# Sampling and feed-forward work redistributed in a fused convolution, attention and feed-forward kernel

## The chip, the cores and the metric

The kernel runs on one core of one Trainium2 chip. Its engines are TensorE (PE, with its weight loads as PEld), VectorE (DVE), ScalarE (ACT), GpSimd (POOL) and SyncE (SP, which here issues most DMAs); each runs its own queue of instructions in order, and they meet at semaphores. The metric is the device time of one execution in microseconds (us), the median of several. Below, "idle" of an engine is time in which its next instruction waits.

## What is computed

The input is four images of 64 x 64 tokens with 256 channels in 32-bit floats. For each image:

```
x = x + deformable_conv(group_norm(x))        # 8 groups x 9 points, bilinear samples, mask, 256x256 out
t = tokens(x)                                 # 4096 x 256
t = t + additive_attention(layer_norm(t))     # alpha = sum_u Wa[u] * tanh(q[u] + k[u] + bh[u]), 32 units
t = t + ffn(layer_norm(t))                    # only the 2047 tokens with the largest weight t.wr + br
                                              # gelu(x w1 + b1) w2 + b2, times that weight
```

The convolution samples by offsets. The kernel splits it into a dense part (for each of 25 window places, a plane of weights times the shifted image, added up) and exact rows for those tokens whose offsets leave the window (gathered one by one).

In the attention the sum over tanh is a function of 4096 x 4096 pairs of tokens. The kernel works it out as sums of quotients: a matmul gives a denominator `d`, ACT takes its logarithm and the exponential of the negative (that is 1/d), another matmul gives a numerator `nn`, DVE multiplies them, and three such products of each pair are added up, before the softmax's own exponential.

The feed-forward sorts the chosen tokens by scattering the rows of all tokens to a table in memory, reads this back in four chunks of 512 rows, runs the two matmuls with the gelu between them, and scatters the results to the output.

## The kernel before

The stages, in the order of the profiled execution: the offsets and weights of all four images (`offsets_and_weights`); the dense sampling of image 0 alone; then for each image n a mixed stage, in which the feed-forward of image n-1, the attention's preparation for n and the first steps of the sampling of n+1 take turns, and the attention of n, which carries the rest of the sampling of n+1 on its DVE; at the end the feed-forward of the last image.

*The attention.* It walks 256 tiles: 8 blocks of 512 queries by 32 blocks of 128 keys. Its order is written by hand in four lanes, one for each engine, with a lag in tiles for each operation. Of one tile, PE makes D1 to D3 (denominators, L878) and N1 to N3 (numerators, L888); ACT takes L1 to L3 (logarithms, L961), E1 to E3 (exponentials, L963) and W (the softmax's exponential, L899); DVE takes six products (L893, "m1a" to "m3b"), "s3b" (L971) and "sum" (L974); POOL takes two additions, "s12" (L967) and "s3a" (L969). After every eight tiles PE multiplies the weights by the values (L915), and DVE adds the result to a running sum ("out", L935). On DVE's lane stand also "side", which in each tile takes one step of the sampling, and "again", which takes a second step in some tiles: as many as there are steps over 256, evenly spread over the tiles.

```
[("m1a", 1), ("m1b", 1), ("m2a", 1), ("side", 0), ("s3b", 2), ("again", 1), ("m2b", 1), ("sum", 2),
 ("m3a", 1), ("m3b", 1), ("out", 3)],
[("s12", 1), ("s3a", 1)],
```

At the end of each block of queries, four "out" slots each finish one row of 128 tokens: the reciprocal (L939), the load of the residual `tr` (L941), the division with its addition (L943), the store (L944), the row's statistics (L746, L747) and its dot product with `wr` (L753), all in one tile (`hand_over`, L922). In the middle of each block, `queries` (L864) makes `qn` for the block after it, two operations of 128x512 on DVE.

*The sampling.* `sample_image` is a generator. One step is a multiply of 128x1024 (L684) or an addition of 128x1024 (L692), each with a `yield` after it. The weight planes `wb` come by DMA (L675). After each quarter of the tokens four pairs of rows go through PE (L705) and out, with an addition of the bias `outb` (L709) and of PE's result (L712) on DVE. When `S.gather` is set, `next(single, None)` advances the generator `exact_rows` inside the multiply's step, so that the gathers on POOL (L618), and the gathered rows' multiply (L629, 128x1152) and reduce (L630), fall into the same tile as the multiply L684. `STEPS` is the number of steps that one image's sampling is taken to have. A single PSUM bank is shared between the values' matmul and the sampling; `bank_taken` tells.

*The feed-forward.* `feed_forward` (L1212) searches the k-th largest weight on DVE, scatters 32 blocks of rows (L1263, POOL's queue), writes the plain rows (`base`, L1276, ACT), and then takes four chunks. A chunk reads its rows `xs` (L1287, POOL's queue), makes `si`, scales the rows into `vs` (L1296, ACT), transposes them into `xT` (L767 and L768), prepares the residual (L1302 on POOL, L1304 on DVE), then runs `ph` (L1312) with the gelu (L1313), and `py` (L1317) with L1320 and the scatter of results (L1324). In the mixed stages its pool "row" has one buffer, so xs, vs and xT are single; in the last feed-forward it has two. `hT`, the gelu's output, has two halves in a tile that takes the place of the tokens' tile once those are read. In the mixed stages the vector operations of the feed-forward and of the preparation go through `pinned`, and show as L257.

*The turns.* A string decides in which order the three generators of a mixed stage advance: m is the feed-forward, o the preparation, s the sampling.

```
turns = "ommm" + "mo" * 5 + "moooo" + "mss" + "oss" * 12 + "m" + ("ossss" * 3 + "msss" * 4) * 4
```

Of the kernel before, what the change touches and what calls it, by code (L numbers as in the profile page):

```python
# [12 lines left out]
ALU = mybir.AluOpType  # L13
# [19 lines left out]
STEPS = 412  # L33
# [12 lines left out]
def layers_kernel(ctx: ExitStack, tc: tile.TileContext, a, out: bass.AP):  # L46
# [51 lines left out]
    tdot = const.tile([P, NT], F32, name="tdot")  # L98
# [134 lines left out]
    S = SimpleNamespace(bank=True, wants=False, gather=True)  # L233
# [327 lines left out]
    def exact_rows(n, uf, out_rows):  # L561

        ui = S.smp.tile([P, 1], I32, tag="ui", name="ui")
# [20 lines left out]
        )  # L584

# [5 lines left out]
        nc.vector.tensor_scalar(pos, pos, 0.0, 65.0, ALU.max, ALU.min)  # L591

# [11 lines left out]
        nc.vector.tensor_copy(ti, gt)  # L604

# [8 lines left out]
        for g in range(G):  # L614
            ga = S.dn.tile([P, K2, 2, 2, CG], F32, tag="ga", name="ga")
            for s in range(K2):
                for dy in range(2):
                    keep(nc.gpsimd.indirect_dma_start(  # L618
                        out=ga[:, s, dy].rearrange("p c e -> p (c e)"), out_offset=None, in_=tab_d[n],
                        in_offset=bass.IndirectOffsetOnAxis(  # L620
                            ap=ti[:, dy, g * K2 + s : g * K2 + s + 1], axis=0
                        ),
                    ))
                yield
            for _ in range(2):
# [4 lines left out]
            keep(nc.vector.tensor_reduce(  # L630
                so[:, g : g + 1, :].rearrange("p g e -> p (g e)"),
                ga.rearrange("p s r c e -> p e (s r c)"), AX.X, ALU.add,
            ))
            yield
# [7 lines left out]
        nc.vector.tensor_copy(sT, pt)  # L642
        pm = S.ps_m.tile([P, C], F32, tag="pm", name="pme")
# [12 lines left out]
    def sample_image(n, depth=1):  # L656
# [3 lines left out]

        uf = yield from list_tokens(n)
# [3 lines left out]
        for c in range(L // CH):  # L665
            ac = S.dn.tile([P, CC, CH], F32, tag="ac", name="ac", bufs=min(depth, 2))
            for f in range(CC):
                xs = S.dn.tile([P, CH // W + 4, MP], F32, tag="xs2", name="xs2", bufs=min(depth, 2))
                o = c * (CH // W) * MP
                nc.sync.dma_start(  # L670
                    out=xs.rearrange("p r w -> p (r w)"), in_=xp_d[n][f, :, o : o + (CH // W + 4) * MP]
                )
                for d in range(ND):
                    wb = S.dn.tile([P, CH], F32, tag="wb", name="wb", bufs=2 * depth)
                    nc.sync.dma_start(  # L675
                        out=wb, in_=wt_d[n][f, d : GH * ND : ND, c * CH : (c + 1) * CH].partition_broadcast(CG)
                    )
# [12 lines left out]
                    yield  # L690
                    if d > 0:
                        keep(nc.vector.tensor_add(ac[:, f, :], ac[:, f, :], pr))  # L692
                        yield
            for i in range(0, CH // P, 2):
                while bank_taken():
                    if S.gather:
                        next(single, None)
                    yield
# [10 lines left out]
                keep(nc.vector.tensor_add(  # L709
# [5 lines left out]
                )  # L715
                yield
        for _ in single:
            yield
        put_rows(n, *exact[0])

# [27 lines left out]

    def weight_sums(i, row):

        row_stats(tmv[:, i, :], row)
        pr = S.sb.tile([P, C], F32, tag="tr", name="pr")
        nc.vector.scalar_tensor_tensor(pr, row, 1.0, wr, ALU.mult, ALU.mult, accum_out=tdot[:, i : i + 1])  # L753
# [96 lines left out]
    def attention(n, v, kf, beside, steps):  # L850
# [8 lines left out]
        def queries(q):  # L859
# [3 lines left out]
            for blk in range(2):  # L863
                nc.vector.tensor_scalar(qn[:, blk, :], qf[:, blk, :], csel[:, blk : blk + 1], None, ALU.mult)  # L864
# [31 lines left out]
        ets, acc, pend, due = {}, {}, [], []  # L896
# [25 lines left out]
        def hand_over():  # L922

            if not due:
                return
# [23 lines left out]
        second = min(max(steps - nb, 0), nb)  # L949
        rs, ds, ns = {}, {}, {}  # L950

        def emit(op, b):

            p = int(op[1]) if op[1:2].isdigit() else 0
# [84 lines left out]
        while pend or due:  # L1039
# [6 lines left out]
    def attention_any(n):  # L1046

        num = nc.values_load(wide[0:1, n : n + 1], min_val=0, max_val=2)
        with tc.If(num > 0), scope(
# [116 lines left out]
            for i in range(NT):  # L1166
                weight_sums(i, v[:, i, :])
# [44 lines left out]
    def feed_forward(n, vec):  # L1212
# [8 lines left out]

        r = inv_std(S.one, tmv[:, :, 1], NT, "lnr2")
# [47 lines left out]

# [13 lines left out]
        hT2 = S.one.tile([P, 2, FF // P, 512], F32, tag="big", name="hT")  # L1284
        for s in range(NSORT // 512):
            xs = S.row.tile([P, 4, C + 4], F32, tag="xs", name="xs")
            get = nc.gpsimd.dma_start(  # L1287
# [6 lines left out]
            vs = S.row.tile([P, 4, C], F32, tag="vs", name="vs")  # L1294
# [12 lines left out]
            yield  # L1307
            hT = hT2[:, s % 2]
            for f in range(FF // P):
# [3 lines left out]
                nc.scalar.activation(hT[:, f, :], ph, AF.Gelu_apprx_tanh, bias=b1[:, f, :])  # L1313
            for t in range(4):
# [13 lines left out]
                if t < 3:  # L1328
                    yield
# [23 lines left out]
    for n in range(NB):  # L1353
        with scope(("att", 1, 0), ("smp", 2, 0), ("dn", 1, 0)):
# [5 lines left out]
            with scope(  # L1360
                ("one", 1, 0), ("two", 2, 0), ("sb", 2, 0), ("row", 1, 0), ("rp", 3, 0),
# [16 lines left out]
            with scope(  # L1378
# [3 lines left out]
                attention(n, v, kf, [sampling], STEPS - turns.count("s") if n + 1 < NB else 0)  # L1382
# [42 lines left out]
```

## Time and profile before

| | |
|---|---|
| median of 3 runs | 10,845.07 us (10,837.85 to 10,854.71) |
| the profiled execution | 10,899.14 us, of which the trace's span is 10,897.4 us |
| busy in the span | PE 9,186.4 us (84%), DVE 8,586.7 (79%), ACT 7,381.2 (68%), POOL 5,001.3 (46%) |
| mean granted TensorE clock | 0.897 |

The profiled execution is one run with the profiler on, and lies 54 us above the median. Windows of it, with times from the span's start:

| stage | from, to (us) | length |
|---|---|---|
| offsets and weights of all images | 0, 812 | 812 |
| sampling of image 0 | 812, 1477 | 665 |
| preparation of attention 0 | 1477, 1580 | 103 |
| attention 0 with sampling of image 1 | 1580, 3657 | 2077 |
| rest of it, then mixed stage 1 | 3657, 4080 | 423 |
| attention 1 with sampling of image 2 | 4080, 6066 | 1986 |
| mixed stage 2 | 6083, 6466 | 383 |
| attention 2 with sampling of image 3 | 6466, 8456 | 1990 |
| mixed stage 3, without sampling | 8473, 8781 | 308 |
| attention 3, without sampling | 8781, 10675 | 1894 |
| feed-forward of image 3 | 10675, 10898 | 223 |

In a group's line of the profile stand the source line, the engine, the operation, output and inputs with their shapes, the count, then the busy time in us and the mean of one in ns, and at the end the engine's idle time just before these instructions and what ended it. In a line of the stage table each engine has its busy time in the window and its number of instructions; then come the granted clock, the DMA's busy share and GB/s.

### The profile page before, as it was taken

The page shows a single profiled execution, that of the slowest core. Times are in us where ns is not written, and L with a number is a line of the kernel's source. Part 1 is how long each engine was busy: PE and PEld are TensorE (multiplying, and loading weights), DVE is VectorE, ACT ScalarE, POOL GpSimd, SP SyncE. Part 2 cuts the span into 40 slices and gives each one's busy share as a digit, 9 for nine tenths or more (in the row PEclk, how much of TensorE's full clock was granted, in tenths as well). Part 3 has the DMA queues.
Part 4 walks back from the last instruction along what each step waited for, and adds up shares of the span by engine and source line. Part 5 has one row for each costly group of instructions (what it writes and reads, how often), then busy time and mean ns, then how long its engine had stood idle before and what let it go on. Part 6 is the DMA issues. An engine that isn't in the chain of part 4 may idle for free. (4 is left out here: it accounts for less than half of the span.)

```text
span 10897.4 us, 115889 instructions
## 1 busy us (share of the span) xinstructions
PE 9186.4 (84%) x38460; PEld 4477.6 (41%) x38460; DVE 8586.7 (79%) x13502; ACT 7381.2 (68%) x8388; POOL 5001.3 (46%) x2947
## 2 busy tenths in 40 slices
PE   7871049999999679999999679999999699999996
PEld 4541014444444344444444344444444344444444
DVE  7767879898999668888888668888888357777772
ACT  4440027777888428888888338888888378888882
POOL 0004216665555316666555226666555145555552
PEclk8985569999999779999999789999999799999998
DMA  3336642221111351222111442212111300000002
GB/s 116 120 130 194 212 141 63 59 63 57 62 57 59 122 160 50 52 51 51 51 50 45 141 129 51 52 49 51 50 50 40 103 13 8 8 8 7 7 5 74
DMA packets 375187, 766.02 MB, mean 70 GB/s; under 512 B 49104, under 2 KB 204400, under 8 KB 374544
## 3 DMA queue, kind: packets, MB, share of 16 engines
q1 hardware_dynamic: 315984, 670.26, 19.1%
q0 software_dynamic: 32448, 54.39, 3.2%
q10 hardware_dynamic: 26112, 33.56, 0.9%
q8 instruction: 310, 5.08, 0.2%
q14 instruction: 333, 2.73, 0.1%
HBM read 580.88 MB, written 177.14 MB: 70 GB/s over the span
## 5 line engine op out<-in xcount | busy, mean ns | idle before, releaser
L893 DVE TENSOR_TENSOR r<-nn,r 128x512 f32<-128x512 f32 x6144 | 3942.0, 682 | 1119.7 <-PE nn L888 1066.9
L888 PE MATMUL nn<-qn,kf 32*128 32x512 f32 (+1 forms) x12288 | 4486.1, 646 | 281.1 <-DVE r L893 243.3
L967 POOL TENSOR_TENSOR r<-r 128x1024 f32<-128x1024 f32 x1024 | 2725.0, 2661 | 3062.9 <-DVE r L893 3003.8
L961 ACT ACTIVATE r<-d 128x1024 f32<-128x1024 f32 x3072 | 3117.8, 1015 | 1269.3 <-DVE r L971 833.4
L878 PE MATMUL d<-qf,kf 32*128 32x512 f32 (+1 forms) x12288 | 3376.3, 638 | 63.7 <-ACT r L961 59.4
L963 ACT ACTIVATE r<-r 128x1024 f32<-128x1024 f32 x3072 | 3124.1, 1051 | 32.6
L915 PE MATMUL pv<-v,et 128*128 128x257 f32 x8192 | 2241.4, 420 | 18.1 <-DVE acv L935 18.1
L888 PEld LDWEIGHTS nn<-qn,kf 32*128 32x128 f32 (+1 forms) x12288 | 1398.8, 188 | 2008.3 <-DVE r L893 1530.7
L915 PEld LDWEIGHTS pv<-v,et 128*128 128x128 f32 x8192 | 1591.4, 204 | 1042.8 <-issue 801.6
L878 PEld LDWEIGHTS d<-qf,kf 32*128 32x128 f32 (+1 forms) x12288 | 1024.9, 187 | 1337.8 <-issue 800.2
L969 POOL TENSOR_TENSOR r<-r 128x512 f32<-128x512 f32 x1024 | 1311.5, 1281 | 184.6 <-DVE r L893 111.9
L692 DVE TENSOR_TENSOR ac<-ac,prd 128x1024 f32<-128x1024 f32 x768 | 968.2, 1261 | 9.4
L684 DVE TENSOR_TENSOR prd<-xs,wb 128x1024 f32<-128x1024 f32 x768 | 954.0, 1242 | 20.9 <-DMA wb<-wt 18.8
L618 POOL DMA_INDIRECT ga<-tab,tii x576 | 660.6, 1147 | 223.8 <-issue 118.6
L899 ACT ACTIVATE et<-et,nshift 128x512 f32<-128x512 f32 x1024 | 723.7, 707 | 26.6 <-DVE et L974 26.6
L971 DVE TENSOR_TENSOR r<-r 128x512 f32<-128x512 f32 x1024 | 699.9, 684 | 2.7 <-POOL r L967 2.6
L974 DVE TENSOR_TENSOR et<-r 128x512 f32<-128x512 f32 x1024 | 696.7, 680 | 3.6 <-POOL r L969 3.5
L116 ACT ACT_TABLE_LOAD x9 | 11.5, 1283 | 844.3 <-DVE mv L257 692.4
L705 PE MATMUL pmo<-outwp,ac 128*128 128x256 f32 x512 | 148.2, 443 | 473.7 <-DVE ac L692 433.6
L1324 POOL DMA_INDIRECT out_dram<-vs,si x64 | 74.6, 1165 | 563.3 <-DVE vs L257 386.5
L478 POOL MEMSET w<- 128x1600 f32 x16 | 22.9, 1432 | 675.0 <-DVE red L454 385.9
L705 PEld LDWEIGHTS pmo<-outwp,ac 128*128 128x128 f32 x512 | 108.4, 221 | 527.3 <-DVE ac L692 315.6
(343 smaller groups left out, 5446.3 us busy)
## 6 DMA issues: line engine op xcount, KB each, us to landing
wb<-wt SPq DMA_DIRECT2D x800, 512.0 KB
tab<-tb SPq DMA_DIRECT2D x128, 256.0 KB
v<-t SPq DMA_DIRECT2D x64, 512.0 KB
xs<-xp SPq DMA_DIRECT2D x32, 680.0 KB
xp<-xp SPq DMA_DIRECT2D x32, 544.0 KB
xt<-in_x_dram SPq DMA_DIRECT2D x32, 512.0 KB
xr<-in_x_dram SPq DMA_DIRECT2D x64, 256.0 KB
t<-xr SPq DMA_DIRECT2D x64, 256.0 KB
```

The source lines that it names most:

```text
L684: keep(nc.vector.tensor_tensor(pr.rearrange("p (r w) -> p r w", w=W), src, wb.rearrange("p (r w) -> p r w", w=W), ALU.mult,))
L692: keep(nc.vector.tensor_add(ac[:, f, :], ac[:, f, :], pr))
L878: keep(nc.tensor.matmul(d[:, j, :], kf[g, blk, rows(kt)], qs[q][0][g, blk, :], start=True, stop=True))
L888: keep(nc.tensor.matmul(nn, kf[g, blk, rows(kt)], qs[q][1][g, blk, :], start=True, stop=True))
L893: keep(nc.vector.tensor_tensor(r[:, j, :], ns[j], r[:, j, :], ALU.mult))
L899: keep(nc.scalar.activation(ets[b], ets[b], AF.Exp, bias=nshift))
L915: keep(nc.tensor.matmul(pv, ets[b0 + i][:, rows(j)], v[:, k0 + i, :], start=(i == 0), stop=(i == PVB - 1)))
L961: keep(nc.scalar.activation(rs[b, p], ds.pop((b, p)), AF.Ln))
L963: keep(nc.scalar.activation(rs[b, p], rs[b, p], AF.Exp, scale=-1.0))
L967: keep(nc.gpsimd.tensor_tensor(rs[b, 1], rs[b, 1], rs[b, 2], ALU.add))
L969: keep(nc.gpsimd.tensor_tensor(rs[b, 1][:, 0], rs[b, 1][:, 0], rs[b, 3][:, 0], ALU.add))
L971: keep(nc.vector.tensor_add(rs[b, 1][:, 1], rs[b, 1][:, 1], rs[b, 3][:, 1]))
```

## The change

1. *Pieces of the sampling.* `exact_rows` yields True where its next piece is to have a step of its own; `sample_image` then runs it after the addition's step (`while own`). The gathered rows' multiply and its reduce, now in two halves, the start of the list and the projection at its end are such pieces. Waiting for the bank no longer advances the gather.
2. *Second steps by what is left.* `S.left` counts the steps that remain, from `STEPS` = 440 (412 before). "again" adds to an account what is left, shared among the tiles left, and takes a second step when this reaches one.
3. *Row ends in pieces.* `hand_over` makes the sum at once, and queues the division and the statistics, which run one at a time in "out" slots that have no sum. `tr` and `tt` have four buffers.
4. *Engines.* `qn` and the addition of `outb` go from DVE to POOL.
5. *The dot product with `wr`* leaves the attention for the start of `feed_forward`, which makes it in 32 operations from the loaded tokens.
6. *The chunks' rows.* A function `chunk(s)` fetches and prepares the rows. xs and vs have two places each inside the large tile, whose hT is now single; chunk s+1 is prepared after the second `py` of chunk s. xs is issued by SP. xT has two buffers in the mixed stages too.
7. *Turns* follow the new yields; the first m, with the loads of the feed-forward, comes before the first o.

```diff
-STEPS = 412
+STEPS = 440
...
+            yield
+            yield True
             gf = ga.rearrange("p s r c e -> p (s r c) e")
             wv = wg[:, g * K2 : (g + 1) * K2].rearrange("p s r (c o) -> p (s r c) o", o=1)
             keep(nc.vector.tensor_tensor(gf, gf, wv.to_broadcast([P, 4 * K2, CG]), ALU.mult))
-            keep(nc.vector.tensor_reduce(
-                so[:, g : g + 1, :].rearrange("p g e -> p (g e)"),
-                ga.rearrange("p s r c e -> p e (s r c)"), AX.X, ALU.add,
-            ))
+            for e in (slice(0, CG // 2), slice(CG // 2, CG)):
+                yield True
+                keep(nc.vector.tensor_reduce(
+                    so[:, g, e], ga[..., e].rearrange("p s r c e -> p e (s r c)"), AX.X, ALU.add,
+                ))
             yield
...
-                    if S.gather:
-                        next(single, None)
+                    S.left -= 1
+                    own = S.gather and next(single, None)
                     yield
                     if d > 0:
                         keep(nc.vector.tensor_add(ac[:, f, :], ac[:, f, :], pr))
+                        S.left -= 1
+                        yield
+                    while own:
+                        own = next(single, None)
+                        S.left -= 1
                         yield
...
-                keep(nc.vector.tensor_add(
+                keep(nc.gpsimd.tensor_add(
                     xr, xr, outb.rearrange("p (o c) -> p o c", o=1).to_broadcast([P, 2, C])
                 ))
...
-                nc.vector.tensor_scalar(qn[:, blk, :], qf[:, blk, :], csel[:, blk : blk + 1], None, ALU.mult)
+                keep(nc.gpsimd.tensor_scalar(qn[:, blk, :], qf[:, blk, :], csel[:, blk : blk + 1], None, ALU.mult))
...
             if not due:
+                if rest:
+                    if len(rest) == late[0]:
+                        late[0] -= 1
+                    rest.pop(0)()
                 return
...
-                es = S.sb.tile([P, 1], F32, tag="es", name="es")
-                nc.vector.reciprocal(es, ac[:, j, C:])
-                tr = S.sb.tile([P, C], F32, tag="tr", name="tr")
+                tr = S.sb.tile([P, C], F32, tag="tr", name="tr", bufs=4)
                 nc.sync.dma_start(out=tr, in_=t_d[n][rows(i)])
-                t2 = S.sb.tile([P, C], F32, tag="tt", name="t2")
-                nc.vector.scalar_tensor_tensor(t2, ac[:, j, :C], es, tr, ALU.mult, ALU.add)
-                nc.sync.dma_start(out=t2_d[n][rows(i)], in_=t2)
-                weight_sums(i, t2)
+                t2 = S.sb.tile([P, C], F32, tag="tt", name="t2", bufs=4)
+
+                def divide():
+                    es = S.sb.tile([P, 1], F32, tag="es", name="es")
+                    keep(nc.vector.reciprocal(es, ac[:, j, C:]))
+                    keep(nc.vector.scalar_tensor_tensor(t2, ac[:, j, :C], es, tr, ALU.mult, ALU.add))
+                    nc.sync.dma_start(out=t2_d[n][rows(i)], in_=t2)
+
+                rest.insert(len(rest) - late[0], divide)
+                rest.append(lambda: row_stats(tmv[:, i, :], t2, pinned))
+                late[0] += 1
...
-            elif op == "side" or op == "again" and (b + 1) * second // nb > b * second // nb:
+            elif op == "side":
                 for side in beside:
                     next(side, None)
+            elif op == "again":
+                second += max(S.left / max(nb - 6 - b, 1) - 1, 0)
+                if second >= 1:
+                    second = min(second - 1, 1)
+                    emit("side", b)
...
+        tdot = S.one.tile([P, NT], F32, name="tdot")
+        for i in range(NT):
+            pr = S.sb.tile([P, C], F32, tag="tte", name="pr")
+            vec.scalar_tensor_tensor(pr, v[:, i, :C], 1.0, wr, ALU.mult, ALU.mult, accum_out=tdot[:, i : i + 1])
+            if i % 8 == 7:
+                yield
...
-        hT2 = S.one.tile([P, 2, FF // P, 512], F32, tag="big", name="hT")
-        for s in range(NSORT // 512):
-            xs = S.row.tile([P, 4, C + 4], F32, tag="xs", name="xs")
-            get = nc.gpsimd.dma_start(
+
+        big = S.one.tile([P, NT * (C + 4)], F32, tag="big", name="big")
+        nh, nx, nv = FF // P * 512, 4 * (C + 4), 4 * C
+        hT = big[:, :nh].rearrange("p (f q) -> p f q", q=512)
+        held = {}
+
+        def chunk(s):
+
+            o = nh + s % 2 * nx
+            xs = big[:, o : o + nx].rearrange("p (t c) -> p t c", t=4)
+            o = nh + 2 * nx + s % 2 * nv
+            vs = big[:, o : o + nv].rearrange("p (t c) -> p t c", t=4)
+            get = nc.sync.dma_start(
...
-                if t < 3:
-                    yield
+                if t == 1 and s + 1 < NSORT // 512:
+                    chunk(s + 1)
+                yield
...
-                ("one", 1, 0), ("two", 2, 0), ("sb", 2, 0), ("row", 1, 0), ("rp", 3, 0),
+                ("one", 1, 0), ("two", 2, 0), ("sb", 2, 0), ("row", 2, 0), ("rp", 3, 0),
...
-                    turns = "ommm" + "mo" * 5 + "moooo" + "mss" + "oss" * 12 + "m" + ("ossss" * 3 + "msss" * 4) * 4
+                    turns = (
+                        "mo" + "m" * 5 + "mo" * 6 + "m" + "ooo" + "s" + "oss" * 2 + "m" + "oss" * 7 + "m" + "oss" * 3
+                        + ("m" + "ossss" * 3 + "msss" * 4) * 4
+                    )
                 else:
-                    turns = "o" * 10 + "ss" + "os" * 24
+                    turns = "o" * 10 + "s" + "os" * 24
...
-                attention(n, v, kf, [sampling], STEPS - turns.count("s") if n + 1 < NB else 0)
+                attention(n, v, kf, [sampling])
```

More of the change, by code (lines that the diff above doesn't have):

```diff
@@ L97, in layers_kernel @@
     tmv = const.tile([P, NT, 2], F32, name="tmv")
-    tdot = const.tile([P, NT], F32, name="tdot")
     wr = load_rows(const, "wr", a["L1_ffn_wr"].rearrange("d o -> (d o)"))
@@ L230, in rows @@
         return slice(i * P, (i + 1) * P)
-    S = SimpleNamespace(bank=True, wants=False, gather=True)
+    S = SimpleNamespace(bank=True, wants=False, gather=True, left=0)
     def bank_taken():
@@ L604, in exact_rows @@
         nc.vector.tensor_copy(ti, gt)
+        yield True
         wg = S.dn.tile([P, GP, 2, 2], F32, tag="wg", name="wg")
@@ L624, in exact_rows @@
                 yield
-            for _ in range(2):
-                yield
+            yield
+            yield True
             gf = ga.rearrange("p s r c e -> p (s r c) e")
@@ L629, in exact_rows @@
             keep(nc.vector.tensor_tensor(gf, gf, wv.to_broadcast([P, 4 * K2, CG]), ALU.mult))
-            keep(nc.vector.tensor_reduce(
-                so[:, g : g + 1, :].rearrange("p g e -> p (g e)"),
-                ga.rearrange("p s r c e -> p e (s r c)"), AX.X, ALU.add,
-            ))
+            for e in (slice(0, CG // 2), slice(CG // 2, CG)):
+                yield True
+                keep(nc.vector.tensor_reduce(
+                    so[:, g, e], ga[..., e].rearrange("p s r c e -> p e (s r c)"), AX.X, ALU.add,
+                ))
             yield
@@ L642, in exact_rows @@
         nc.vector.tensor_copy(sT, pt)
+        yield True
+        while bank_taken():
+            yield True
         pm = S.ps_m.tile([P, C], F32, tag="pm", name="pme")
@@ L656, in sample_image @@
     def sample_image(n, depth=1):
+        S.left = STEPS
         uf = yield from list_tokens(n)
@@ L695, in sample_image @@
                 while bank_taken():
-                    if S.gather:
-                        next(single, None)
                     yield
@@ L715, in sample_image @@
                 )
+                S.left -= 1
                 yield
         for _ in single:
+            S.left -= 1
             yield
         put_rows(n, *exact[0])
+        S.left = 0
     def sample_any(n):
@@ L747, in row_stats @@
         vec.bn_aggr(mv, st)
[L749 to L753, printed above, removed]
     def load_tokens(v, src):
@@ L848, in attention_prep, with attention @@
         vec.tensor_copy(wide[:, n : n + 1], lo[:, 0:1])
-    def attention(n, v, kf, beside, steps):
+    def attention(n, v, kf, beside):
         keep(nc.scalar.preload_act_table_set("natural_log_exp_and_others"))
@@ L893, in quotient @@
             keep(nc.vector.tensor_tensor(r[:, j, :], ns[j], r[:, j, :], ALU.mult))
-        ets, acc, pend, due = {}, {}, [], []
+        ets, acc, pend, due, rest, late = {}, {}, [], [], [], [0]
         def weigh(b):
@@ L937, in hand_over @@
                 i = 4 * q + j
-                es = S.sb.tile([P, 1], F32, tag="es", name="es")
-                nc.vector.reciprocal(es, ac[:, j, C:])
-                tr = S.sb.tile([P, C], F32, tag="tr", name="tr")
+                tr = S.sb.tile([P, C], F32, tag="tr", name="tr", bufs=4)
                 nc.sync.dma_start(out=tr, in_=t_d[n][rows(i)])
-                t2 = S.sb.tile([P, C], F32, tag="tt", name="t2")
-                nc.vector.scalar_tensor_tensor(t2, ac[:, j, :C], es, tr, ALU.mult, ALU.add)
-                nc.sync.dma_start(out=t2_d[n][rows(i)], in_=t2)
-                weight_sums(i, t2)
+                t2 = S.sb.tile([P, C], F32, tag="tt", name="t2", bufs=4)
[7 more added lines that the diff above has]
+                late[0] += 1
         queries(0)
         nb = NQ * NT
-        second = min(max(steps - nb, 0), nb)
+        second = 0.0
         rs, ds, ns = {}, {}, {}
         def emit(op, b):
+            nonlocal second
             p = int(op[1]) if op[1:2].isdigit() else 0
@@ L1038, in attention @@
         assert not any(lanes)
-        while pend or due:
+        while pend or due or rest:
             hand_over()
@@ L1166, in attention_any @@
             for i in range(NT):
-                weight_sums(i, v[:, i, :])
+                row_stats(tmv[:, i, :], v[:, i, :])
     def kth_largest(wa, vec):
@@ L1293, in feed_forward @@
             vec.tensor_scalar(si, xs[:, :, C + 3], float(n * L), None, ALU.add)
-            vs = S.row.tile([P, 4, C], F32, tag="vs", name="vs")
             for t in range(4):
@@ L1306, in feed_forward @@
                 )
-            yield
-            hT = hT2[:, s % 2]
+            held[s] = xs, vs, si, xT
+        chunk(0)
+        yield
+        for s in range(NSORT // 512):
+            xs, vs, si, xT = held.pop(s)
             for f in range(FF // P):
@@ L1313, in feed_forward @@
                 nc.scalar.activation(hT[:, f, :], ph, AF.Gelu_apprx_tanh, bias=b1[:, f, :])
+            yield
             for t in range(4):
@@ L1327, in feed_forward @@
                 )
-                if t < 3:
-                    yield
+                if t == 1 and s + 1 < NSORT // 512:
+                    chunk(s + 1)
+                yield
     with scope(
```

## The prediction

> **What bounds the kernel now.** I read the stage table first (windows cut at the stage borders), because the busy shares of the whole span mix stages with different limits. The first columns are the window and its length, then the busy time and instruction count of PE, PEld, DVE, ACT and POOL.
>
> ```profile
> 1580.00:3657.00 2077.00, 1955.45 (x8297) 913.82 (x8298) 1859.97 (x2780) 1648.63 (x1792) 1182.61 (x657) 0.94 0.22 60
> 4080.00:6066.00 1986.00, 1883.68 (x8264) 869.30 (x8264) 1749.10 (x2693) 1646.49 (x1792) 1158.22 (x654) 0.96 0.18 50
> 6083.00:6466.00 383.00, 240.88 (x705) 141.99 (x706) 243.76 (x458) 98.58 (x144) 68.81 (x62) 0.71 0.52 169
> 8473.00:8781.00 308.00, 211.04 (x606) 118.51 (x606) 86.66 (x254) 101.02 (x146) 58.21 (x57) 0.75 0.27 90
> 8781.00:10675.00 1894.00, 1820.50 (x8192) 834.18 (x8192) 1378.66 (x2384) 1666.70 (x1792) 1010.59 (x513) 0.97 0.02 7
> 10675.00:10898.00 223.00, 125.25 (x444) 84.61 (x444) 46.96 (x163) 49.40 (x83) 60.39 (x56) 0.77 0.26 87
> ```
>
> Four attentions take 7,950 of 10,897 us. Attention 3, with no sampling beside it, is 183 us shorter than attention 0; ACT's busy time hardly differs (1,667 against 1,649), DVE's does: 1,379 against 1,860. Next, the groups inside attention 1 (4200 to 6000):
>
> ```profile
> L893 DVE TENSOR_TENSOR r<-nn,r 128x512 f32<-128x512 f32 x1404 | 901.0, 683 | 196.1 <-PE nn L888 188.2 <-ACT r L963 5.9 <-PE d L878 0.3
> L961 ACT ACTIVATE r<-d 128x1024 f32<-128x1024 f32 x702 | 712.3, 1015 | 289.6 <-DVE r L971 229.8 <-PE d L878 37.9 <-PE nn L888 13.6
> L967 POOL TENSOR_TENSOR r<-r 128x1024 f32<-128x1024 f32 x234 | 623.8, 2666 | 686.4 <-DVE r L893 670.3 <-issue 11.7 <-ACT r L963 4.3
> L969 POOL TENSOR_TENSOR r<-r 128x512 f32<-128x512 f32 x234 | 300.2, 1283 | 36.3 <-DVE r L893 19.6 <-POOL r L967 0.2
> L753 DVE SCALAR_TENSOR_TENSOR pr<-t,wr 128x256 f32<-128x256 f32 x28 | 24.6, 877 | 0.0
> L630 DVE TENSOR_REDUCE so<-ga 128x32 f32<-128x1152 f32 x8 | 17.0, 2119 | 0.3
> L864 DVE TENSOR_SCALAR qn<-qf,csel 128x512 f32<-128x512 f32 x12 | 14.8, 1274 | 0.0
> L709 DVE TENSOR_TENSOR xr<-xr,outb 128x512 f32<-128x512 f32 x8 | 6.8, 849 | 0.0
> ```
>
> Each of 256 tiles needs on ACT 3 x 1.015 (logarithm, L961) + 3 x 1.051 (exponential, L963) + 0.707 (softmax weight, L899) = 6.91 us: a floor. ACT loses 229.8 us to DVE's add L971, so DVE sets what lies above it. POOL waits 670/234 = 2.9 us per tile for DVE. In the timeline I took the distance from one add L974 (a tile's last) to the next. Its median is 7.82 in attention 0 and 6.95 in the others: the ACT floor. The mean is 7.99, 7.64, 7.66, 7.27; over 255 intervals the excess above 6.95 is 264, 175, 180 and 80 us. That is all an easier vector side can win in the loops.
>
> The excess by what a tile carries: one step of sampling, 6.95 (DVE work 6.11 to 6.44); two steps, 8.09, the next tile catching up with 6.46, so +0.65 per second step; attention 0 (three steps per two tiles), 7.15 on average; end-of-block tiles with division, statistics and dot product, 8.7 to 9.9, 32 per image, with late tiles after them; gather tiles with L629 and L630 together, 10.4 to 13.3, 8 per image; tiles with qn, 7.9 to 9.8. So it is uneven vector work, more than its sum, that breaks the floor.
>
> Last, the feed-forward of image 0 in its mixed stage (3741 to 4080):
>
> ```profile
> L1302 POOL TENSOR_TENSOR vs<-vs,xs 128x1024 f32<-128x1024 f32 x4 | 10.0, 2494 | 69.0 <-ACT qe L822 46.0 <-PE ptt L767 23.0
> L767 PE MATMUL ptt<-ident,vs 128*128 128x128 f32 x32 | 8.8, 403 | 34.5 <-ACT vs L1296 34.5
> L1296 ACT ACTIVATE vs<-xs 128x256 f32<-128x256 f32 x16 | 8.4, 590 | 75.0 <-DMA xs<-sort 50.6 <-DVE si L257 24.3
> ```
>
> The rows of a chunk are fetched only when the chunk before has let go of their single buffer: wait for xs, then for the transposes, then work.
>
> **What the Trainium skill says.** (1) GPSIMD Engine Reference, 4.1 Engine selection: two-input elementwise work is about twice as slow on GpSimd, one-input work about line rate. The trace agrees for two inputs: the 128x512 add is 1.283 us on POOL (L969) and 0.684 on DVE (L971). (2) SBUF — State Buffer, "SBUF: two separate sides": VectorE and GpSimd share a port pair, and whichever starts first holds it for the whole instruction. The trace fits: the dot product L753 takes 0.97 us in attention 0 and 0.41 in attention 3, qn L864 1.40, 1.27 and 0.92 in attentions 0, 1 and 3. Work taken off DVE is thus priced at its slow value.
>
> **The change, part by part.** Prices are of the profiled execution (10,899.14 us, span 10,897.4), which lies 54 us above the median of the runs, 10,845.07.
>
> *Vector work that leaves the attentions.* qn, 16 per image: 16 x 1.40 = 22.4 us (attention 0), 20.4, 20.4, 14.7. The dot product with its accumulator read, 32 per image: 32 x 1.043 = 33.4, then 32 x 0.955 = 30.6 twice, 32 x 0.49 = 15.7. outb add, 16 per image sampled: 18.9 (1.18 each), 13.6, 13.6. Sums 75, 65, 65, 30.
>
> *What POOL gets.* qn on POOL is not shown; nearest is the 128x512 two-input add, 1.28 us, and as one input less it may be 0.6. Both fit in the 2.9 us for which POOL waits each tile. Queued behind qn and the outb add on POOL are the sums L967 and L969, for which DVE and then ACT wait; a block has 2 qn in one tile (2.6 us, inside the gap). The outb add also waits for its DMA xr; SP issues that after the pair before has been stored, a tile (7 us) earlier. Cost taken 0; if the cover fails, 112 items of up to 1.3 us, +145 us.
>
> *Pieces with their own slots.* Gather multiply and two half reduces (estimate 1.06 each, half of 2.12) take three tiles instead of one of 3.47 us; the division, store and statistics wait for "out" slots without a sum. STEPS rises by 28, so second steps grow: 440 - 121 - 256 = 63 for images 2 and 3 against 34 before, about 159 against 130 for image 1, now spread by what is left, and nothing remains after the loop.
>
> *Attention 0.* DVE work is 1,860 - 75 + about 20 from the 33 us of sampling that follow the loop now = 1,805, or 7.05 per tile; the present pattern needs 0.31 more than its own work (7.15 for 6.84), so 7.36 x 255 = 1,877, plus an estimated 48 for tiles with division or statistics beside two steps: 1,925 against 2,037, **-112**. The leftover goes: **-33**.
>
> *Attentions 1 and 2.* DVE has (1,749 - 65)/256 = 6.6 us per tile, under the floor. 255 x 6.95 = 1,772, plus 69 seconds (63 and some small pieces) x 0.65 = 45, plus 56 (about a third of today's excess) for irregular tiles: 1,873 against 1,948 and 1,953. **-75 each**, and the leftovers, 9 us each, **-18**.
>
> *Attention 3.* (1,379 - 30)/256 = 5.3 us; nothing beside it. Floor 1,772 + 18: 1,790 against 1,853, **-63**.
>
> *Mixed stages 1 and 2 (383 us).* Between chunks DVE is idle, in the first of the two, 26.8 us for xs, 11.7 for transposes, 4.1 for L1302: about 42, to which 10 at the first chunk come. Earlier fetching saves these, less what other work already fills. Added: the dot product, 32 x 0.49 = 15.7 us on DVE, which must wait for v2's load, and with it the search for the k-th largest and the scattered writes come some 19 us later. Net **-25 each**. xs is now issued by SP, behind whatever waits there for wb; from nothing to +15 each, taken 0.
>
> *Mixed stage 3.* PE's three waits of 6.9 us go (-20), the dot product is exposed (+19): **0**. *Last feed-forward.* It was double-buffered already; the dot product lies on the path (+15), first transposes and three waits of 1.3 us save 5: **+10**. *Sampling of image 0.* The outb add leaves DVE, 16 x 0.68 less waits: **-5**.
>
> Sum: -5 - 112 - 33 - 50 - 150 - 18 + 0 - 63 + 10 = **-421**, 3.9% of 10,899. Off the median: 10,845 - 421 = 10,424; I take 10,430.
>
> **Rivals.**
> - *A, the forecast*, 10,430. Own range 10,345 to 10,530: 50 us on attention 0, 30 on each of the next two, 25 on the last and 20 on each boundary do not all fall one way.
> - *B, only the sum counts.* DVE's removed work is won, 235 us, but spreading wins nothing, since a second step still costs 0.65 and there are 29 more per image (3 x 19 = 57); the boundaries give their leftovers (51) but nothing in the rows, and the last stage costs 10: -235 + 57 - 51 + 10 = -219, so 10,626. For it: attention 0 stays DVE-bound. Against: the one-step tiles already run at the floor.
> - *C, everything reaches the floor.* Attentions at 1,772 (1,850 for the first, a DVE sum without gaps): -187 - 176 - 181 - 81 - 51 and the boundaries as in A (-45): -721 plus the block ends that cannot vanish, about 130: 10,255. Against: catch-up tiles have cost 0.65 each.
> - *D, POOL becomes the gate: slower.* qn and the outb add stand in order before the sums. To cancel 421 us and add 22, 112 items must each delay a tile by 4 us, that is take 4 + 2.9 = 6.9 us. It decides from there on; at 8 us each they cost 112 x 5.1 = 571, and 571 - 421 gives 10,995. For it: the operation is not in the trace. Against: five times the nearest row.
> - *E, rows are not fetched early* (SP blocked, or the buffer inside the large tile frees late): two boundaries lose their 25 each and gain up to 10: 10,500, inside A's range.
>
> **How the numbers follow.** A with E 0.60, B 0.20, C 0.10, D 0.07, an even result from some mixture 0.03. The range 10,320 to 10,650 holds A and B and leaves out C's core, D and the even case: 0.2. The runs lie within 17 us of each other, so 0.2%, 22 us, is about what can be told from no change. Faster: A, B, C, 0.90; same 0.03; slower, D, 0.07.
>
> **What would show it.** Intervals of L974: mean near 7.5, 7.35, 7.35, 7.0; no pair of L629 and L630 in one tile; POOL's wait before L967 falling by about what it took over, with ACT's wait before L961 shrinking. If POOL's sums start late with DVE waiting for L967, D holds. In the mixed stages the waits for xs and for L1296 should go. If intervals with two steps stay above 8 without a catch-up, B holds; a stage of the feed-forward that grows by more than 20 us would make my dot-product term wrong.

## The result: 18% slower, and where the time went

The changed kernel takes 12,800.43 us (median of 4 runs, 12,791.64 to 12,806.06) against 10,842.89 us before: ratio 1.1803, 95% interval 1.1782 to 1.1823. The forecast was 10,430 us. Its profiled execution has a span of 12,789.9 us.

The changed kernel's stage table, windows cut as before (window and length; busy us and count of PE, PEld, DVE, ACT, POOL; clock; DMA share; GB/s):

```profile
1590.00:3570.00 1980.00, 1924.03 (x8216) 877.53 (x8214) 1826.97 (x2680) 1641.18 (x1786) 1246.84 (x683) 0.97 0.22 65
3607.00:3950.00 343.00, 218.30 (x706) 134.33 (x706) 258.51 (x517) 101.77 (x147) 72.35 (x58) 0.77 0.56 185
3960.00:6990.00 3030.00, 2601.31 (x8186) 1139.17 (x8186) 1701.17 (x2587) 3000.56 (x2806) 1177.22 (x680) 0.80 0.12 33
7380.00:10410.00 3030.00, 2610.85 (x8188) 1141.58 (x8190) 1701.97 (x2585) 3000.52 (x2806) 1177.62 (x680) 0.80 0.12 33
10737.00:12550.00 1813.00, 1772.79 (x8186) 807.81 (x8183) 1363.54 (x2293) 1665.85 (x1792) 1034.43 (x528) 1.00 0.02 7
12556.00:12790.00 234.00, 125.41 (x444) 84.73 (x444) 58.39 (x224) 50.03 (x83) 57.20 (x52) 0.75 0.24 82
```

Attentions 0 and 3 became shorter. Attentions 1 and 2 went from 1,986 and 1,990 us to 3,030 each, and ACT, 1,646 us busy in them before, is busy for 3,000, with about a thousand instructions more. The groups of the page name them, DVE's product of the kernel before first, then the changed kernel's:

```profile
L893 DVE TENSOR_TENSOR r<-nn,r 128x512 f32<-128x512 f32 x6144 | 3942.0, 682 | 1119.7 <-PE nn L888 1066.9
```

```profile
L904 DVE TENSOR_TENSOR r<-nn,r 128x512 f32<-128x512 f32 x6144 | 3942.7, 682 | 3168.0 <-PE nn L899 2394.2
L889 PE MATMUL d<-qf,kf 32*128 32x512 f32 (+1 forms) x12288 | 3600.0, 677 | 357.0 <-ACT r L983 312.9
L983 ACT ACTIVATE r<-d 128x1024 f32<-128x1024 f32 x3072 | 3073.8, 1018 | 490.1 <-DVE r L993 289.6
L983 ACT ACT_TABLE_LOAD x1024 | 1313.8, 1283 | 125.3 <-PE d L889 54.8
L985 ACT ACT_TABLE_LOAD x1024 | 1313.8, 1283 | 18.3
```

The page of before has nine table loads among its listed groups; here stand 2,048 more, one for each switch between logarithm (L983) and exponential (L985). There are four in each of 512 tiles, because the order L2 L1 E2 E1 L3 E3 W changes function four times. DVE's product L904 shows the other side: its idle time has risen from 1,120 us to 3,168 us, and reads as a wait for PE. PE's denominators (L889) in turn wait 313 us for ACT's logarithm (L983). The releaser named in a group's line is the next link and not the cause.

The granted clock of these two attentions fell as well, from 0.96 before to 0.80. It isn't what made them long: ACT is busy for 99% of them (3,000 of 3,030 us), and its logarithm takes as long as before (1,018 ns on average, before 1,015). With the loads gone (experiment 1) the clock is 0.99 in attention 1.

ACT's timeline at the end of the first mixed stage of the changed kernel (start, length, engine, line, operation, idle before):

```profile
3892.65 1.28 ACT L1357 ACT_TABLE_LOAD   x1
3893.94 1.48 ACT L1357 ACTIVATE big<-ph,b 128x512 f32<-128x512 f32 x2
...
3896.70 0.69 ACT L1357 ACTIVATE big<-ph,b 128x512 f32<-128x512 f32 x1 [1.28 <-PE ph L1356]
3897.41 1.28 ACT L867 ACT_TABLE_LOAD   x1
3898.70 1.28 ACT L1357 ACT_TABLE_LOAD   x1
3899.99 1.26 ACT L1357 ACTIVATE big<-ph,b 128x512 f32<-128x512 f32 x2
...
3959.07 1.28 ACT L983 ACT_TABLE_LOAD   x1 [54.81 <-PE d L889]
3960.36 1.94 ACT L983 ACTIVATE r<-d 128x1024 f32<-128x1024 f32 x2
3962.32 1.28 ACT L985 ACT_TABLE_LOAD   x1
3963.61 2.00 ACT L985 ACTIVATE r<-r 128x1024 f32<-128x1024 f32 x2
3965.63 1.28 ACT L983 ACT_TABLE_LOAD   x1
```

L867 is the attention's `preload_act_table_set`, of the one set with both functions. The last four gelus (L1357) come after it and load their own set over it. Nothing loads the common set again, and from then on a load stands at each change between L983 and L985. The trace doesn't name the sets; that each function then brings one of its own is the reading, and experiment 2 tests it. The Trainium skill describes such sets (ScalarE: Activation LUTs, "Table sets: the hidden batching unit": ln then exp needs one load, since one set has both), and the kernel before agrees: its trace has 4 loads at the preload and none at the logarithm or the exponential. In attention 0 no gelu lies in the way; in the third mixed stage the gelus happen to stand before L867.

### The profile page after: what moved, and what is told of

Read it like the earlier page. It is cut to its first block, busy times and chain, and to the rows that moved or that the text cites. A ratio compares the mean times of both kernels' runs of the same rounds, so it can differ in the third digit from the quotient of the medians.

```text
span 12789.9 us, 117986 instructions
## 1 busy us (share of the span) xinstructions
PE 10537.9 (82%) x38460; PEld 4969.4 (39%) x38460; DVE 8505.9 (67%) x13406; ACT 10110.9 (79%) x10439; POOL 5174.4 (40%) x3059
## 5 line engine op out<-in xcount | busy, mean ns | idle before, releaser
L904 DVE TENSOR_TENSOR r<-nn,r 128x512 f32<-128x512 f32 x6144 | 3942.7, 682 | 3168.0 <-PE nn L899 2394.2
L899 PE MATMUL nn<-qn,kf 32*128 32x512 f32 (+1 forms) x12288 | 4607.1, 664 | 591.7 <-DVE r L904 564.6
L889 PE MATMUL d<-qf,kf 32*128 32x512 f32 (+1 forms) x12288 | 3600.0, 677 | 357.0 <-ACT r L983 312.9
L983 ACT ACTIVATE r<-d 128x1024 f32<-128x1024 f32 x3072 | 3073.8, 1018 | 490.1 <-DVE r L993 289.6
L985 ACT ACTIVATE r<-r 128x1024 f32<-128x1024 f32 x3072 | 3128.7, 1051 | 27.8
L927 PE MATMUL pv<-v,et 128*128 128x257 f32 x8192 | 2755.3, 494 | 14.9 <-DVE acv L951 14.9
L927 PEld LDWEIGHTS pv<-v,et 128*128 128x128 f32 x8192 | 1906.6, 244 | 1307.1 <-issue 948.7
L899 PEld LDWEIGHTS nn<-qn,kf 32*128 32x128 f32 (+1 forms) x12288 | 1424.5, 196 | 2437.8 <-DVE r L904 1811.8
L889 PEld LDWEIGHTS d<-qf,kf 32*128 32x128 f32 (+1 forms) x12288 | 1061.1, 196 | 2148.3 <-ACT r L983 1296.8
```

The costliest lines, as they stand in the source:

```text
L889: keep(nc.tensor.matmul(d[:, j, :], kf[g, blk, rows(kt)], qs[q][0][g, blk, :], start=True, stop=True))
L899: keep(nc.tensor.matmul(nn, kf[g, blk, rows(kt)], qs[q][1][g, blk, :], start=True, stop=True))
L904: keep(nc.vector.tensor_tensor(r[:, j, :], ns[j], r[:, j, :], ALU.mult))
L927: keep(nc.tensor.matmul(pv, ets[b0 + i][:, rows(j)], v[:, k0 + i, :], start=(i == 0), stop=(i == PVB - 1)))
L983: keep(nc.scalar.activation(rs[b, p], ds.pop((b, p)), AF.Ln))
L985: keep(nc.scalar.activation(rs[b, p], rs[b, p], AF.Exp, scale=-1.0))
```

## The experiments

Where a kernel is called "mended", it is the changed kernel with the first edit below. Ratios are to the kernel before on the same chip, with 95% intervals. Three chips were used. The kernel before took 10,873.52 us on the first (experiments 1 and 2, and the first two parts of experiment 4), 10,838.31 us on the second (experiment 3 and the other three parts of experiment 4) and 10,844.46 us on the third (experiment 5). Times of two chips are compared by their ratios.

**1. The loads taken away.**

```diff
-                nc.scalar.activation(hT[:, f, :], ph, AF.Gelu_apprx_tanh, bias=b1[:, f, :])
+                S.gelu = nc.scalar.activation(hT[:, f, :], ph, AF.Gelu_apprx_tanh, bias=b1[:, f, :])
...
-        keep(nc.scalar.preload_act_table_set("natural_log_exp_and_others"))
+        table = keep(nc.scalar.preload_act_table_set("natural_log_exp_and_others"))
+        if n:
+            tc.add_manual_dep(table.ins, S.gelu.ins.name, ...)
```

> Theory T (the table loads are the whole loss): with the preload of the attention's table tied behind the last gelu, the ACT row of table loads in attentions 1 and 2 is gone (2,048 loads of 1.283 us), their intervals fall from 11.85 us to 7.3 to 7.4, and the time comes to 10,445 us, between 10,380 and 10,520. Rival P (the work moved to POOL, or the pieces, slow attentions 1 and 2 by themselves, and the loads only fill ACT's gaps): the intervals stay above 9 us and the time above 11,500 us.

10,565.57 us; ratio 0.9717 (0.9701 to 0.9733). The trace has no load at the logarithm or the exponential any more (they are L988 and L990 here), attentions 1 and 2 have mean intervals of 7.43 and 7.42 us, and theory T holds: the one misplaced preload turns a change worth -2.8% into +18%. The time itself missed its expectation, 10,380 to 10,520 us. Taken on 10,843 us the ratio gives 10,536 us, 106 us above the likeliest case's time and 6 us beyond its own range; experiments 4 and 5 look into that.

**2. The loads added to the kernel before.**

```diff
-        keep(nc.scalar.preload_act_table_set("natural_log_exp_and_others"))
+        if n in (0, 3):
+            keep(nc.scalar.preload_act_table_set("natural_log_exp_and_others"))
```

> The kernel before with the preload left out for images 1 and 2, nothing else. Theory T: the same four loads per tile appear and attentions 1 and 2 go to intervals of about 11.85 us, so the time is 10,843 + 2 x (3,022 - 1,950) = 12,990 us, between 12,900 and 13,050. Rival P: the loads alone are mostly hidden in ACT's idle time, under 12,000 us.

13,046.48 us, inside the expected 12,900 to 13,050; 1.1999 (1.1975 to 1.2023). Its page has the same two groups:

```profile
L962 ACT ACT_TABLE_LOAD x1024 | 1313.8, 1283 | 75.5 <-PE d L879 57.5
L964 ACT ACT_TABLE_LOAD x1024 | 1313.8, 1283 | 18.4
```

Both loops take 3,022 and 3,024 us, as the changed kernel's two do (3,022 and 3,021), though its vector work is arranged quite differently. With ACT at its limit, all that the change did on DVE is worth nothing there.

**3. Why the gelus got behind the preload.** `keep` ties an instruction to the one recorded just before it on the same engine, and to no other. In both strings of turns the last group is m, ossss three times, then msss four times. Before, its first m recorded the chunk's rows, and the gelu came with the second m. Now the rows are recorded earlier and the gelu has a yield of its own, so that the first m records it and three turns of the preparation follow. The last ACT instruction before the preload is then the preparation's, and nothing ties the gelus.

```diff
-                        + ("m" + "ossss" * 3 + "msss" * 4) * 4
+                        + ("ossss" * 3 + "m" + "msss" * 4) * 4
```

> The changed kernel with one edit, in the string of turns: in each of the four groups the feed-forward's gelu turn comes after the preparation's turns and not before. Theory T2 (the preload is tied only to the ACT instruction that was recorded last before it, which the new turns made the preparation's, so four gelus got behind the preload): the last gelus again stand before the preload, the loads in attentions 1 and 2 are gone, and the time is that of the mended kernel, 0.972 of before, within 40 us. Rival (the order on ACT comes from the chunk's new place for its rows): loads stay, about 12,800 us.

10,526.22 us; 0.9713 (0.9696 to 0.9729). Moving one letter in the group removes the loads, so theory T2 holds; the new place of the chunk's rows isn't the cause. The ratio is that of the mended kernel.

By the traces the two full mixed stages are 22 and 17 us shorter than the mended kernel's. The edit is hardly the reason. The mended kernel's trace has three waits for a signal whose sender the profile doesn't show ("remote"; columns: sum, times, longest, in us):

```profile
DVE oh L550 <- remote: 54.6, 10, 8.1
ACT qe L833 <- remote: 19.1, 1, 19.1
DVE mm L257 <- remote: 17.8, 1, 17.8
```

The traces of before and of all four kernels of the first chip have such waits. Those of the changed kernel, which has the same instructions at L550, and of the other two chips have none; what sends the signal stays open. Stages are therefore compared only between traces of one kind: the first chip's with the mended kernel's, the second and third chips' with this experiment's (it differs from the mended kernel in the place of the gelus).

**4. The parts of the rest, undone one at a time in the mended kernel.**

qn and the outb add back on DVE:

```diff
-                keep(nc.gpsimd.tensor_scalar(qn[:, blk, :], ...))
+                nc.vector.tensor_scalar(qn[:, blk, :], ...)
...
-                keep(nc.gpsimd.tensor_add(
+                keep(nc.vector.tensor_add(
```

> The mended kernel with qn and the outb add back on DVE. If POOL hides them and DVE is what they cost: slower than the mended kernel by 40 to 130 us, most of it in attention 0. Rival D (they hold up the sums on POOL): faster than the mended kernel by 20 us or more.

10,578.57 us; 0.9728 (0.9712 to 0.9745): 13 us above the mended kernel on the same chip, inside the intervals. Neither expectation came true; since nothing was won, rival D is excluded. The groups of the mended kernel's attention 1 (4100 to 5800) tell why:

```profile
L988 ACT ACTIVATE r<-d 128x1024 f32<-128x1024 f32 x686 | 695.1, 1014 | 226.5 <-DVE r L998 186.9 <-PE d L894 17.7 <-PE nn L904 10.0
L994 POOL TENSOR_TENSOR r<-r 128x1024 f32<-128x1024 f32 x229 | 604.0, 2638 | 551.1 <-DVE r L909 541.3 <-ACT r L990 4.3 <-issue 3.1
L880 POOL TENSOR_SCALAR qn<-qf,csel 128x512 f32<-128x512 f32 x12 | 23.8, 1985 | 0.0
L723 POOL TENSOR_TENSOR xr<-xr,outb 128x512 f32<-128x512 f32 x8 | 10.2, 1270 | 0.0
L726 DVE TENSOR_TENSOR xr<-pmo,xr 128x512 f32<-128x512 f32 x8 | 5.5, 692 | 17.2 <-PE pmo L719 8.6 <-POOL r L996 8.6
```

POOL still waits 541/229 = 2.4 us a tile for DVE. But L726 waits 17.2 us for PE's projection and for POOL, and 7.2 us with the addition on DVE, where the eight additions take 10.1 us. DVE is spared the work and waits as long for it, and in attentions 1 and 2 the tile with xr takes 10.1 us either way. With qn on DVE its tile, one of 32, takes 9.3 us, yet the loops of attentions 1 and 2 grow by only 2 and 3 us, so the tiles after it catch up.

The gather's pieces in one step:

```diff
-                    own = S.gather and next(single, None)
-                    yield
+                    own = S.gather and next(single, None)
+                    while own:
+                        own = next(single, None)
+                    yield
```

(with the later `while own` loop left out, and STEPS 412)

> The mended kernel with the gather's pieces run inside the multiply's step again (the reduce stays in halves) and STEPS back at 412. If spreading the heavy tiles is worth what the tiles of 10 to 13 us suggest: 8 such tiles per image at +3 to 4 us, three images, so 60 to 110 us slower than the mended kernel. Rival B (only the sum counts): within 20 us of it, since the number of second steps falls by the same work.

10,644.53 us; 0.9791 (0.9774 to 0.9807), 79 us above the mended kernel on the same chip: as expected from spreading. By stages, 15 us of it lie ahead of attention 0, and 25, 21 and 20 in the three attentions that carry sampling.

The row ends at once:

```diff
-                rest.insert(len(rest) - late[0], divide)
-                rest.append(lambda: row_stats(tmv[:, i, :], t2, pinned))
-                late[0] += 1
+                divide()
+                row_stats(tmv[:, i, :], t2, pinned)
```

> The mended kernel with division and statistics again in the tile of their sum. If uneven tiles cost what the prediction says: 32 end tiles per image at 8 us and more, 100 to 200 us slower than the mended kernel over four images, 15 to 40 of it in attention 3. Rival B (only the sum counts): within 30 us.

10,673.56 us; 0.9849 (0.9833 to 0.9866), 147 us above experiment 3 on the same chip, as expected from uneven tiles. Loops by the traces: +21, +40, +42 and +52 us; in attention 3 that is more than the expected 15 to 40. Spreading again, not the sum: the same instructions run.

The next rows fetched late:

```diff
-                if t == 1 and s + 1 < NSORT // 512:
+                if t == 3 and s + 1 < NSORT // 512:
```

> The mended kernel with the next chunk's rows fetched after the chunk's last py and not after its second. If the early fetch is what shortens the mixed stages: 10 to 25 us slower in each of three, 15 to 20 in the last feed-forward, together 50 to 100 us. Rival E (the fetch is not early in effect, or other work fills the wait): within 20 us.

10,593.33 us; 0.9776 (0.9759 to 0.9792). That is 67 us above experiment 3 on the same chip. ACT's group in the first mixed stage, experiment 3's first (3602 to 3982), then this one's (3608 to 3960):

```profile
L1336 ACT ACTIVATE big<-big 128x256 f32<-128x256 f32 x16 | 8.6, 590 | 19.5 <-DMA big<-sort 15.4 <-DVE vT L257 4.0
```

```profile
L1341 ACT ACTIVATE big<-big 128x256 f32<-128x256 f32 x16 | 8.5, 592 | 77.6 <-DMA big<-sort 75.4 <-DMA out_dram<-big,si 2.1
```

The wait comes back, 75 us where 15 was. By the traces the first two mixed stages are 28 and 34 us longer, about half of the added wait; the third and the last feed-forward hardly change (+0.3 and +2.5). The sum lies in the expected 50 to 100, but it is spread otherwise: more in the first two stages, and nothing in the third. Rival E is excluded.

The dot product back in the attention:

```diff
+    def weight_sums(i, row, vec=nc.vector):
+        row_stats(tmv[:, i, :], row, vec)
+        pr = S.sb.tile([P, C], F32, tag="tte", name="pr")
+        vec.scalar_tensor_tensor(pr, row, 1.0, wr, ALU.mult, ALU.mult, accum_out=tdot[:, i : i + 1])
...
-                rest.append(lambda: row_stats(tmv[:, i, :], t2, pinned))
+                rest.append(lambda: weight_sums(i, t2, pinned))
```

(with the 32 operations at the start of `feed_forward` left out)

> The mended kernel with the dot product made again in the attention, as part of the statistics' piece. By the prediction's terms the attentions lose 15 to 35 us each (sum 80) and the four feed-forwards win 15 to 19 each (sum 70): between 40 us faster and 50 us slower than the mended kernel. Rival: in pieces it hides in the attentions, then 40 to 70 us faster.

10,633.73 us; 0.9816 (0.98 to 0.9832), 108 us above experiment 3 on the same chip, where between 40 us won and 50 us lost had been expected; the rival, a gain, is excluded. By the traces the loops take +36, +20, +13 and +17 us (sum 86), the mixed stages +14, +18 and +5, the last feed-forward -14. So no mixed stage becomes shorter without the dot product, though 19 us each had been charged for it; why they become longer stays open. In the last feed-forward of the changed kernel it is:

```profile
L1252 DVE SCALAR_TENSOR_TENSOR pr<-v,wr 128x256 f32<-128x256 f32 x32 | 11.6, 421 | 3.6 <-DMA v<-t 3.5
L1252 DVE DVE_READ_ACCUMULATOR pr<-v,wr 128x1 f32 x32 | 2.6, 81 | 0.0
```

0.42 us apiece with no POOL instruction running at their start. In the trace of before, in attention 0, 7 of the 32 began so and took 0.41 us, and 25 began while POOL was in an instruction and took 1.03.

**5. The second steps,** both in the kernel of experiment 3. First the old even spread:

```diff
-                second += max(S.left / max(nb - 6 - b, 1) - 1, 0)
-                if second >= 1:
-                    second = min(second - 1, 1)
-                    emit("side", b)
...
+            elif op == "again" and (b + 1) * second // nb > b * second // nb:
+                emit("side", b)
```

(with `second` set at the loop's start to the steps left over 256)

> The kernel with the turns mended and the second steps again evenly spread, as many as the steps left at the attention's start over 256 (159 for image 1, 63 for images 2 and 3). If the account by what is left does the work: steps that wait for the bank or have nothing to do leave a rest after each loop, 10 to 30 us per image, 20 to 90 us slower than 0.9713 of before. Rival: the two rules give nearly the same tiles, within 20 us.

10,524.88 us; 0.9706 (0.9689 to 0.9722): the same time. The loops are shorter (1,941, 1,879 and 1,874 us for 1,982, 1,889 and 1,892), and the stages after them longer by 40, 15 and 11: what the account by what is left wins behind the loop it pays in the loop. The time is the rival's, though not for its reason, since the tiles do differ.

Then no second steps in attentions 1 and 2:

```diff
-                if second >= 1:
+                if second >= 1 and n == 0:
```

> The kernel with the turns mended, and no second steps in attentions 1 and 2; what is left of the sampling runs after the loop. Measures a second step's price: at the prediction's 0.65 us the loops shorten by 60 x 0.65 = 39 us each, at 1.05 us (two-step tiles without a catch-up) by 63 us each. The rest after the loop, 60 steps at 1.25 us or more, adds 75 to 110 us each, so the whole is slower by 20 to 140 us.

10,589.82 us; 0.9765 (0.9745 to 0.9784). The loop of attention 1 falls from 1,889.1 to 1,819.6 us with about 60 fewer two-step tiles: 1.16 us for each, against 0.65 in the sum. The rest after it takes 102.9 us more, 1.7 us for each step, so a second step is still the cheaper place. In all, 56 us are lost by the ratios, as expected (20 to 140).

## Why the prediction was wrong

*The step that failed* is the floor, 6.91 us of ACT in each tile. It was read from the kernel before and carried into all four attentions of the changed one as if ACT's instructions there were given; further table loads were put at nothing, without a reason. In attentions 1 and 2 four loads of 1.283 us come to it, 5.13 us a tile: ACT is busy for 3000.56/256 = 11.72 us a tile, and the mean interval rose from 7.64 and 7.66 to 11.85. None of the rivals had ACT becoming slower; the slower one named POOL. The part that did it, the gelu's own yield with the turns that follow the new yields, was not priced at all: of a moved step the prediction counted DVE work and DMA, and not what else on ACT is tied to it. The order of ACT's instructions is fixed when the kernel is built, so this could have been counted beforehand: 2,129 table loads in the trace of after, 78 in that of before.

*The floor without the loads* was misread too. It adds the means of instructions that overlap: in the timeline above two logarithms in a row take 1.94 us together. ACT is busy for 1646.49/256 = 6.43 us a tile in attention 1 of the kernel before, and the prediction's own catch-up tiles of 6.46 us lie below its floor. In the mended kernel's attention 3, whose tiles come 6.95 us apart in the median, ACT still has gaps (9000 to 10200, 171 tiles):

```profile
9000.00:10200.00 1200.00, 1178.97 (x5472) 538.07 (x5472) 915.81 (x1544) 1113.60 (x1197) 690.36 (x353) 1.00 0.02 7
L988 ACT ACTIVATE r<-d 128x1024 f32<-128x1024 f32 x513 | 521.4, 1016 | 80.9 <-PE d L894 45.7 <-DVE r L998 14.9
```

PE is busy for 98% of this window, ACT for 93%, and ACT's gaps are mostly waits for PE's denominators. So PE seems to set the 6.95 us, and that it agrees with 6.91 was luck. No run tests this.

*The other terms, read in the mended kernel* (against the span of before, 10,897; forecast -421, by traces -336, by timed runs -308):

| term | forecast us | measured us |
|---|---|---|
| attention 0's loop | -112 | -56 |
| loops of attentions 1 and 2 | -75 each | -54, -59 |
| attention 3's loop | -63 | -73 |
| boundaries 0/1, 1/2, 2/3 | -58, -34, -9 | -51, -30, -38 |
| last feed-forward | +10 | +17 |
| up to attention 0 | -5 | +6 |

Mean intervals and counts of attention 0, worked out from the distance of its last additions in the traces of before and of the mended kernel:

| tiles of attention 0 | before | mended |
|---|---|---|
| one step | 101 of 6.80 us | 44 of 6.67 |
| two steps | 97 of 8.44 | 109 of 7.95 |
| row end beside one or two steps | 24 of 8.7 to 9.9 | 49 of 7.0 to 8.2 |
| gather | 7 of 10.6 to 11.7 | 17 of 7.2 to 8.0 |
| xr | 12 of 10.60 | 16 of 10.23 |

- That it is "uneven vector work, more than its sum" was right: gather and row ends lose their peaks, undoing either costs 79 and 147 us, and attention 3's loop comes within 8 us of the 1,772 us counted as its floor.
- Attention 0 won half of what was forecast. The likely reason is the term of 0.31 us for three steps in two tiles: pieces with their own slots make more two-step tiles, 151 for 109, each 1.3 us longer than a one-step tile, with too few light tiles left to catch up. The price of 0.65 for a second step came from a kernel with 34 of them, and was 1.16 in attention 1 here. How much of the miss is due to this isn't shown.
- qn and the outb addition, 124 us of priced work on DVE, were worth about 13. (The price was a little high: 78 us for qn, whose 64 instructions take 66 in the trace of before, since some fall where POOL is idle.) The forecast took it that POOL needs at most 1.28 us for qn, perhaps 0.6. It needs 1.57 us in the median of 64, up to 3.09, and 1.985 on average in the window above; one fits the gap of 2.9 us, two don't.
- The dot product's move was worth 108 us in all, 86 of it in the loops, where 110 us of work had been priced (all of it takes 104 in the trace of before); its charge of 19 us per mixed stage was wrong (nothing was lost there), the 15 at the end right (14).
- The early rows cut the waits as said: undoing them costs 67 us, 28 and 34 in the two full mixed stages. The forecast had 25 each after the dot product's charge of 19, that is 44 for the rows.

What stays open: the xr tiles, 10.1 to 10.2 us each and hardly moved (10.5 to 10.6 before); no kernel that places PE's projection elsewhere was tried.

## What to carry to other kernels

Before summing what each engine gains, check for hidden state that lives between instructions: an activation table that one preload sets for thousands of instructions is lost to a single later instruction of another set. When instructions are moved between generators, list for every pinned instruction which one is now recorded before it, and count the table loads in ACT's order. Evening out heavy tiles paid here (79 and 147 us). Taking work off an engine paid only in part: 108 us for the dot product, about 13 for qn and the outb addition together. And before two traces are compared stage by stage, look in both for waits that no instruction of the kernel explains.

## What the runs showed of the hardware

A table load takes 1.283 us each time, and stood between activations without overlap; in the timeline above the next activation starts 0.01 us after it, so a switch costs about 1.3 us here. The Trainium skill gives the same 1.283 us and another 1.38 us of drain per switch (ScalarE: Activation LUTs, "What ACT_TABLE_LOAD costs"); the traces show no such drain between back-to-back switches, and 1,024 loads lengthened an attention by 1,074 us, 1.05 us each, less than a load takes, since ACT had idled for part of each tile before (busy 6.43 us of 7.64, then 11.72 of 11.85). A one-input operation with a per-partition scalar, 128x512, took 1.55 us at least and 1.57 in the median on POOL, more than the two-input addition of the same size at 1.27. A multiply with accumulation, 128x256, took 0.41 us on DVE when no POOL instruction was running at its start, and 1.03 in attention 0 when one was.
